# A program order planned by one clock per engine, PSUM banks held by hand, and ScalarE's reads moved, in a stack of four graph layers

## The chip, the cores and the metric

The kernel runs on one core of one Trainium2 chip. A core has five engines that work side by side, each through its own instruction stream in order: TensorE (PE in the profile, its weight loads PEld) multiplies matrices and writes to PSUM, an accumulation memory of eight banks; VectorE (DVE), ScalarE (ACT) and GpSimd (POOL) work element by element; SyncE (SP) starts transfers. All but PSUM data lies in the on-chip memory SBUF. The metric is the device time of one execution in microseconds (us), the median of several runs. Everything is float32.

## The reference, cut to what matters

There are 64 batches of 256 nodes with 128 features, and one 256 x 256 matrix `adj`. Each of four layers normalises its input over the features, takes the positive part, and adds the layer's result to its input.

```python
def _L0_gnn_ref(input, in_matrix, out_matrix, ...):          # both matrices are adj
    def step(h, _):
        m_in = einsum('nm,bmd->bnd', in_matrix, h); m_out = einsum('nm,bmd->bnd', out_matrix, h)
        av = concatenate([m_in, m_out], -1)
        u3 = h @ u3_w.T + u3_b
        z = sigmoid(av @ w3_w.T + w3_b + u3)
        r = sigmoid(av @ w4_w.T + w4_b + u3)
        hv = tanh(av @ w5_w.T + w5_b + (r * h @ u5_w.T + u5_b))
        return (1.0 - z) * h + z * hv, None
    # ... five steps
def _L1_gnn_ref(X, A1, A2, Theta1, bias):                    # both matrices are adj
    # x1 = A^T x0, x2 = 2 A^T x1 - x0 for each matrix
    # ... out = relu([X, x1, x2, x1, x2] @ Theta1 + bias)
def _L2_gnn_ref(x, adj, weight, bias):
    y = einsum('bnf,fo->bno', einsum('nm,bmf->bnf', adj, x) + x, weight) + bias
    return y / maximum(sqrt(sum(y * y, 2)), EPS)
def _L3_gnn_ref(x, W, b_lin, a, bias):                       # W and bias are adj
    s1 = einsum('bkf,ef->bke', x, W[:, :F]); s2 = einsum('bkf,ef->bke', x, W[:, F:])
    pre = s1[:, :, None, :] + s2[:, None, :, :] + b_lin
    h = where(pre >= 0, pre, ALPHA * pre)
    e = einsum('bije,e->bij', h, a) + bias
    return sigmoid(einsum('bij,bjf->bif', softmax(e, 2), x))
# each layer: h = maximum(layernorm(x), 0); x = x + layer(h)
```

The last layer is by far the largest: `pre` has 256 x 256 x 256 elements for each batch, one for every pair of nodes and every one of 256 features.

## The kernel before

Two batches, a pair, are worked on together; there are 32 pairs. The last layer of a pair takes 64 slots. In a slot n, four rows i of each half of the nodes are handled with all nodes j, for the 256 features in two blocks of 128. The first block's `max(s2, -s1)` comes from VectorE (`rl_v`). The second block's `relu(s1 + s2)` comes in two of three slots as a sum on GpSimd and a relu on ScalarE (`rl_g`), and in every third slot from eight activations on ScalarE (`rl_s`). TensorE multiplies each of them by the vector `a` (`scores`) into one PSUM bank per half pair.

```python

    def make_sum(n):
        if n >= NPAIR * SLOTS or n % 3 == 0:
            return
        ops = READY[where(n)[0]]
        TILES[n, 1] = relu_pool.tile([P, 4, NB, N], F32, name="rl_g", bufs=6)
        nc.gpsimd.tensor_add(TILES[n, 1], *operands(n, ops[4], ops[6]))
    def make(n):
        if n >= NPAIR * SLOTS:
            return
        p, ic, r = where(n)
        ops = READY[p]
        if ops[5] is None:
            ops[5] = ps_s.tile([P, NB, N], F32, name="s2a")
            project(ops[5], [(adj_t[:, 1, 0:P], ops[2])])
        TILES[n, 0] = relu_pool.tile([P, 4, NB, N], F32, name="rl_v", bufs=5)
        nc.vector.tensor_tensor(TILES[n, 0], *operands(n, ops[3], ops[5]), op=OP.max)
        if n % 3:
            t = TILES[n, 1].rearrange("p g b n -> p (g b n)")
            nc.scalar.activation(t, t, AF.Relu)
        else:
            TILES[n, 1] = relu_pool.tile([P, 4, NB, N], F32, name="rl_s", bufs=2)
            for g in range(4):
                for b in range(NB):
                    i = ic * P + g * 32 + r
                    nc.scalar.activation(TILES[n, 1][:, g, b, :], ops[6][:, b, :], AF.Relu,
                                         bias=ops[4][:, b, i:i + 1], scale=1.0)
    def scores(n):
        p, ic, r = where(n)
        if r == 0:
            PE[0] = ps_e.tile([P, NB, N], F32, name="pe")
            project(PE[0], [(g2, READY[p][2])], stop=False)
        for k in range(NE):
            rl = TILES.pop((n, k))
            for g in range(4):
                nc.tensor.matmul(flat(PE[0])[g * 32:(g + 1) * 32, :], win[:, k, 31 - r:63 - r], flat(rl[:, g]),
                                 start=False, stop=(r == 31 and k == NE - 1), skip_group_check=True)
```

While a pair goes through its slots, the layers before it of the next two pairs are computed a step at a time (`front`), and its softmax and output afterwards (`tail`). These are generators: each `yield` ends a step and gives its rough work on TensorE, VectorE and ScalarE.

```python
    def inverse_root(t, op, value):
        nc.gpsimd.tensor_scalar(t, t, value, None, op0=op)
        nc.gpsimd.tensor_tensor(t, t, minus_half, op=OP.pow)
    def norm(src, h):
        stats = work.tile([P, NB * NC, 6], F32, name="stats")
        mv = work.tile([P, NB * NC, 2], F32, name="mv")
        s = src.rearrange("p b c d -> p (b c) d")
        for k in range(NB * NC):
            nc.vector.bn_stats(stats[:, k, :], s[:, k, :])
        for k in range(NB * NC):
            nc.vector.bn_aggr(mv[:, k, :], stats[:, k, :])
        yield 0, 1.3, 0
        inverse_root(mv[:, :, 1], OP.add, LN_EPS)
        yield 0, 0, 0
        pn = bank([P, NB * NC, D], "pn")
        for k in range(NB * NC):
            nc.vector.tensor_scalar(pn[:, k, :], s[:, k, :], mv[:, k, 0:1], mv[:, k, 1:2],
                                    op0=OP.subtract, op1=OP.mult)
        yield 0, 1.6, 0
        nc.scalar.activation(h.rearrange("p b c d -> p (b c) d"), pn, AF.Relu)
        yield 0, 0, 0.6
    # ...
    def side_by_side(o, w, t, start, stop):
        for g in range(0, P, 32):
            nc.tensor.matmul(o[g:g + 32], w[:, g:g + 32], t, start=start, stop=stop, skip_group_check=True)
    def project(pp, pairs, start=True, stop=True):
        for k, (w, t) in enumerate(pairs):
            side_by_side(flat(pp), w, flat(t), start and k == 0, stop and k == len(pairs) - 1)
        return pp
    # ... front(p): norm(x0), then the first layer
        for step in range(STEPS):
            if step:
                pm = mix_nodes(h, adj_t, "pm")
                yield 1.9, 0, 0
                mT = feat("mT", **SHORT)
                nc.scalar.copy(mT, pm)
                yield 0, 0, 0.6
            pr = project(bank([P, NB, N], "pr"), [(u3t, hT), (w4t, mT)])
            yield 1.9, 0, 0
            r = bank([P, NB, N], "r")
            nc.scalar.activation(r, pr, AF.Tanh, bias=br, scale=0.5)
            yield 0, 0, 0.65
            rh = feat("rh", **SHORT)
            nc.vector.scalar_tensor_tensor(rh, r, 1.0, hT, op0=OP.add, op1=OP.mult)
            project(pr, [(w34, mT)], start=False)
            yield 0.9, 0.7, 0
            nc.scalar.activation(pr, pr, AF.Tanh, bias=bz, scale=0.5)
            pv = project(bank([P, NB, N], "pv"), [(w5t, mT), (u5t, rh)])
            yield 1.9, 0, 0.65
            nc.scalar.activation(pv, pv, AF.Tanh, bias=bh, scale=1.0)
            yield 0, 0, 0.65
            d = feat("d", **SHORT)
            nc.vector.tensor_sub(d, pv, hT)
            yield 0, 0.7, 0
            nc.vector.scalar_tensor_tensor(pr, pr, 1.0, d, op0=OP.add, op1=OP.mult)
            hT_new = feat("hT", bufs=4)
            nc.vector.scalar_tensor_tensor(hT_new, pr, 0.5, hT, op0=OP.mult, op1=OP.add)
            hT = hT_new
            yield 0, 1.4, 0
            pt = to_token(hT, "pt")
            yield 0.6, 0, 0
            if step < STEPS - 1:
                h = tok("h", **SHORT)
                # ... copy to h; then x1 and the second layer
        pt = to_feature(h, "pt")
        yield 0.6, 0, 0
        hT = feat("hT", bufs=4)
        nc.scalar.copy(hT, pt)
        pm = mix_nodes(h, adj_n, "pm")
        yield 1.9, 0, 0.6
        c1T = feat("c1T", **SHORT)
        nc.scalar.copy(c1T, pm)
        yield 0, 0, 0.6
        pt = to_token(c1T, "pt")
        yield 0.6, 0, 0
        c1 = tok("c1", **SHORT)
        nc.scalar.copy(c1, pt)
        yield 0, 0, 0.6
        pm = mix_nodes(c1, adj_n, "pm")
        yield 1.9, 0, 0
        c2T = feat("c2T", **SHORT)
        nc.vector.scalar_tensor_tensor(c2T, pm, 2.0, hT, op0=OP.mult, op1=OP.subtract)
        yield 0, 0.7, 0
        po = project_token([(hT, th[:, 0, :]), (c1T, th[:, 1, :]), (c2T, th[:, 2, :])], "po")
        # ... the third layer; then the projections for the fourth
        p1 = project(bank([P, NB, N], "p1"), [(adj_t[:, 0, P:2 * P], hT)])
        p2 = project(bank([P, NB, N], "p2"), [(adj_t[:, 1, P:2 * P], hT)])
        yield 1.9, 0, 0
        s2b = feat("s2b")
        nc.scalar.copy(s2b, p2)
        s1b = feat("s1b")
        nc.scalar.activation(s1b, p1, AF.Identity, bias=blin[:, 1:2], scale=1.0)
        yield 0, 0, 1.3
        p1 = project(bank([P, NB, N], "p1"), [(adj_t[:, 0, 0:P], hT)])
        yield 0.9, 0, 0
        s1n = feat("s1n")
        nc.scalar.activation(s1n, p1, AF.Identity, bias=nblin[:, 0:1], scale=-1.0)
        READY[p] = [x3, h3, hT, s1n, s1b, None, s2b]
```

What stands where in the program is decided slot by slot. A step is put in when it is late against an even pace, or when its work fits under three levels that each slot drains. PSUM comes from pools: five banks that circulate, one for `s2a`, two for the scores.

```python
    ps = ctx.enter_context(tc.tile_pool(name="ps", bufs=5, space=PSUM))
    ps_s = ctx.enter_context(tc.tile_pool(name="ps_s", bufs=1, space=PSUM))
    ps_e = ctx.enter_context(tc.tile_pool(name="ps_e", bufs=2, space=PSUM))
    # ...
    RATE, ROOM = (1.1, 0.65, 0.6), (2.7, 1.8, 1.5)
    level = [0.0, 0.0, 0.0]
    def fits(work):
        return all(l + w <= r or w == 0 for l, w, r in zip(level, work, ROOM))
    def charge(work):
        for k in range(3):
            level[k] += work[k]
    def background(n):
        p, k = n // SLOTS, n % SLOTS + 1
        total = len(WORK)
        room = SLOTS - SUM_AHEAD - 3
        due = {p + 1: half + (total - half) * min(1.0, k / room), p + 2: half * k / SLOTS}
        due = {q: d for q, d in due.items() if q < NPAIR and q not in READY}
        late = {q: d - FRONTS.get(q, (0, 0))[1] for q, d in due.items()}
        if k >= room and p + 1 in late:
            while p + 1 not in READY:
                charge(step(p + 1))
            late.pop(p + 1)
        if tails:
            t = tails[0]
            if n - t[1] > 2 * t[2] + 2 or n - t[1] > 2 * t[2] and fits(t[3]):
                work = next(t[0], None)
                if work is None:
                    tails.pop(0)
                else:
                    charge(work)
                    t[2:] = [t[2] + 1, work]
                in_order()
        for q in sorted(late, key=lambda q: -late[q]):
            work = WORK[FRONTS.get(q, (0, 0))[1]]
            if late[q] > 6 or late[q] > -4 and fits(work):
                charge(step(q))
        for k in range(3):
            level[k] = max(0.0, level[k] - RATE[k])
    # ...
    for n in range(NPAIR * SLOTS):
        background(n)
        make_sum(n + SUM_AHEAD)
        make(n + AHEAD)
        in_order()
        scores(n)
        in_order()
        if n % 32 == 31:
            p, ic, _ = where(n)
            tails.append([tail(p, ic, PE[0], *READY[p][:2]), n, 0, (0, 0.7, 0)])
```

Of the kernel before, what the change touches and what calls it, by code (L numbers as in the profile page):

```python
# [15 lines left out]
NB = 2  # L16
# [4 lines left out]
ENGINES = (mybir.EngineType.PE, mybir.EngineType.DVE, mybir.EngineType.Activation, mybir.EngineType.Pool)  # L21
# [6 lines left out]
def kernel(  # L28
# [49 lines left out]

    nc = tc.nc
# [9 lines left out]
    ps = ctx.enter_context(tc.tile_pool(name="ps", bufs=5, space=PSUM))  # L89
    ps_s = ctx.enter_context(tc.tile_pool(name="ps_s", bufs=1, space=PSUM))  # L90
    ps_e = ctx.enter_context(tc.tile_pool(name="ps_e", bufs=2, space=PSUM))

    def bank(shape, name):
        return ps.tile(shape, F32, tag="bank", name=name)
# [46 lines left out]

    def load_transposed(w, name, scale=None):
# [39 lines left out]
    nc.vector.tensor_copy(th[:, 0, :], th_raw[:, 0, :])  # L182
    nc.vector.tensor_add(th[:, 1:3, :], th_raw[:, 1:3, :], th_raw[:, 3:5, :])

# [38 lines left out]
    def norm(src, h):  # L223

        stats = work.tile([P, NB * NC, 6], F32, name="stats")
        mv = work.tile([P, NB * NC, 2], F32, name="mv")
        s = src.rearrange("p b c d -> p (b c) d")
        for k in range(NB * NC):
            nc.vector.bn_stats(stats[:, k, :], s[:, k, :])  # L229
        for k in range(NB * NC):  # L230
            nc.vector.bn_aggr(mv[:, k, :], stats[:, k, :])  # L231
        yield 0, 1.3, 0
        inverse_root(mv[:, :, 1], OP.add, LN_EPS)
        yield 0, 0, 0
        pn = bank([P, NB * NC, D], "pn")
        for k in range(NB * NC):
            nc.vector.tensor_scalar(pn[:, k, :], s[:, k, :], mv[:, k, 0:1], mv[:, k, 1:2],  # L237
                                    op0=OP.subtract, op1=OP.mult)
        yield 0, 1.6, 0
        nc.scalar.activation(h.rearrange("p b c d -> p (b c) d"), pn, AF.Relu)  # L240
        yield 0, 0, 0.6

    def to_feature(h, name):

        pt = bank([P, NB, NC, P], name)
        for b in range(NB):
            for c in range(NC):
                nc.tensor.transpose(pt[:, b, c, :], h[:, b, c, :], ident)
        return pt.rearrange("p b c n -> p b (c n)")

    def to_token(ht, name):

        pt = bank([P, NB, NC, P], name)
        for b in range(NB):
            for c in range(NC):
                nc.tensor.transpose(pt[:, b, c, :], ht[:, b, c * P:(c + 1) * P], ident)  # L256
        return pt

    def mix_nodes(h, a, name):

        pm = bank([P, NB, N], name)
        for b in range(NB):
            for c in range(NC):
                side_by_side(pm[:, b, :], h[:, b, c, :], a[:, c, :], c == 0, c == NC - 1)
        return pm
# [4 lines left out]
    def side_by_side(o, w, t, start, stop):  # L270

        for g in range(0, P, 32):
            nc.tensor.matmul(o[g:g + 32], w[:, g:g + 32], t, start=start, stop=stop, skip_group_check=True)  # L273

    def project(pp, pairs, start=True, stop=True):

        for k, (w, t) in enumerate(pairs):
            side_by_side(flat(pp), w, flat(t), start and k == 0, stop and k == len(pairs) - 1)
        return pp

    def project_token(pairs, name):

        pp = bank([P, NB, NC, D], name)
        for b in range(NB):
            for c in range(NC):
                for k, (t, w) in enumerate(pairs):
                    nc.tensor.matmul(pp[:, b, c, :], t[:, b, c * P:(c + 1) * P], w,
                                     start=(k == 0), stop=(k == len(pairs) - 1))
        return pp
# [6 lines left out]

    SHORT = dict(tag="short", bufs=14)

    def add_row(po, row):

        t = po.rearrange("p b c d -> p (b c) d")
        nc.vector.tensor_add(t, t, row.unsqueeze(1).to_broadcast([P, NB * NC, D]))
# [3 lines left out]
    def front(p):  # L306

        x0 = XIN.pop(p)
# [3 lines left out]
        yield from norm(x0, h)  # L312
        pt = to_feature(h, "pt")
        yield 0.6, 0, 0
        hT = feat("hT", bufs=4)
        nc.scalar.copy(hT, pt)
        pm = mix_nodes(h, adj_t, "pm")
        yield 1.9, 0, 0.6
        mT = feat("mT", **SHORT)
        nc.scalar.copy(mT, pm)  # L320
        yield 0, 0, 0.6
        for step in range(STEPS):
            if step:
                pm = mix_nodes(h, adj_t, "pm")
                yield 1.9, 0, 0
                mT = feat("mT", **SHORT)
                nc.scalar.copy(mT, pm)
                yield 0, 0, 0.6
            pr = project(bank([P, NB, N], "pr"), [(u3t, hT), (w4t, mT)])
            yield 1.9, 0, 0  # L330
            r = bank([P, NB, N], "r")
            nc.scalar.activation(r, pr, AF.Tanh, bias=br, scale=0.5)  # L332
            yield 0, 0, 0.65
            rh = feat("rh", **SHORT)
            nc.vector.scalar_tensor_tensor(rh, r, 1.0, hT, op0=OP.add, op1=OP.mult)  # L335
            project(pr, [(w34, mT)], start=False)
            yield 0.9, 0.7, 0
            nc.scalar.activation(pr, pr, AF.Tanh, bias=bz, scale=0.5)
            pv = project(bank([P, NB, N], "pv"), [(w5t, mT), (u5t, rh)])
            yield 1.9, 0, 0.65  # L340
            nc.scalar.activation(pv, pv, AF.Tanh, bias=bh, scale=1.0)
            yield 0, 0, 0.65

            d = feat("d", **SHORT)
            nc.vector.tensor_sub(d, pv, hT)  # L345
            yield 0, 0.7, 0
            nc.vector.scalar_tensor_tensor(pr, pr, 1.0, d, op0=OP.add, op1=OP.mult)  # L347
            hT_new = feat("hT", bufs=4)
            nc.vector.scalar_tensor_tensor(hT_new, pr, 0.5, hT, op0=OP.mult, op1=OP.add)  # L349
            hT = hT_new  # L350
            yield 0, 1.4, 0
            pt = to_token(hT, "pt")
            yield 0.6, 0, 0
            if step < STEPS - 1:
                h = tok("h", **SHORT)
                nc.scalar.copy(h, pt)  # L356
                yield 0, 0, 0.6
        x1 = tok("x1")
        nc.vector.tensor_add(x1, x0, pt)
        yield 0, 0.7, 0  # L360
# [3 lines left out]
        yield from norm(x1, h)  # L364
        pt = to_feature(h, "pt")
        yield 0.6, 0, 0
        hT = feat("hT", bufs=4)
        nc.scalar.copy(hT, pt)
        pm = mix_nodes(h, adj_n, "pm")
        yield 1.9, 0, 0.6  # L370
        c1T = feat("c1T", **SHORT)
        nc.scalar.copy(c1T, pm)
        yield 0, 0, 0.6
        pt = to_token(c1T, "pt")
        yield 0.6, 0, 0
        c1 = tok("c1", **SHORT)
        nc.scalar.copy(c1, pt)
# [261 lines left out]
```

## Time and profile before

| | |
|---|---|
| time, median of 3 runs | 5768.48 us (5767.91 to 5768.98) |
| span of the profiled execution | 5767.0 us |
| mean granted TensorE clock | 0.985 |
| GpSimd: 1365 sums `rl_g`, 3624 ns each | 4907.8 us busy |
| VectorE: 2048 `rl_v`, 2280 ns each | 4580.8 us busy |
| VectorE: 512 `pn` (the end of the norm), 412 ns each | 210.9 us busy |
| ScalarE: 1365 relus `rl_g`, 1923 ns each | 2588.1 us busy |
| ScalarE: 5464 activations `rl_s`, 516 ns each | 2262.3 us busy |
| ScalarE: 128 relus `h` from `pn`, 597 ns each | 76.5 us busy |

Busy time is the time in which at least one instruction of a group runs. Successive instructions of an engine overlap at their ends, so a mean length is longer than what one instruction costs; the distance between starts tells that. The lengths of TensorE's matmuls are modelled.

In the profile's lines an entry such as `L504 DVE TENSOR_TENSOR rl_v<-s2a,s1n` is a line of the kernel, an engine, an operation, and what is written from what. A wait is put down to the instruction whose end released it.

### The profile page before, as it was taken

Reading aid. Unit: us, or ns where it says so; the run is one execution under the profiler, and the core shown is the slowest. Engines: PE = TensorE matmul, PEld = TensorE weight load, DVE = VectorE, ACT = ScalarE, POOL = GpSimd, SP = SyncE. Lnnn points to the kernel's source line nnn. Section 1 sums busy time; section 2 is a strip of 40 time slices with the busy share of each in tenths; the row PEclk is TensorE's granted clock in tenths of the full one; section 3 lists DMA queues with packets and bytes.
Section 4 is the critical chain, followed back from the end, with each engine's and each line's share of the span. In section 5 each row is a group of like instructions: output and inputs, shape, how many; then the busy total and the mean of one; then the engine's idle time right before and its main releaser. Section 6 shows DMA issues by size and latency. Waiting matters only on the chain.

```text
span 5767.0 us, 121947 instructions
## 1 busy us (share of the span) xinstructions
PE 5395.0 (94%) x51853; PEld 1880.1 (33%) x51853; DVE 5482.7 (95%) x4766; ACT 5432.0 (94%) x8494; POOL 5179.1 (90%) x1819
## 2 busy tenths in 40 slices
PE   6899999999999999999999999999999999999988
PEld 2333333333333333333333333333333333333322
DVE  3999999999999999999999999999999999999998
ACT  2999999999999999999999999999999999999999
POOL 0999899999999999999998999989989999999998
PEclk9999999999999999999999999999999999999999
DMA  0000000000000000000000000000000000000000
GB/s 17 4 4 5 2 5 5 4 5 5 2 5 5 4 5 2 5 5 4 5 5 2 5 5 4 5 2 5 5 4 5 5 2 5 5 3 3 2 3 4
DMA packets 38739, 25.90 MB, mean 4 GB/s; under 512 B 3505, under 2 KB 38193, under 8 KB 38193
## 3 DMA queue, kind: packets, MB, share of 16 engines
q1 hardware_dynamic: 35088, 17.05, 1.0%
q8 instruction: 406, 6.65, 0.5%
q10 hardware_dynamic: 3104, 1.05, 0.1%
q14 instruction: 141, 1.15, 0.1%
HBM read 9.70 MB, written 8.39 MB: 3 GB/s over the span
## 4 chain that ended last, share of the span: by engine, by line
DVE 54%; PE 24%; ACT 11%; issue 7%; POOL 3%; DMA 0%; ACTq 0%; POOLq 0%; SPq 0%; DVEq 0%
DVE rl_v L504 41%; PE pe L525 14%; ACT rl_s L513 4%; ACT rl_g L507 4%; PE pm L273 3%; DVE pn L237 3%; PE pr L273 2%; POOL rl_g L493 2%; PE p L273 2%; DVE stats L229 1%; DVE hT L349 1%; DVE rh L335 1%; DVE d L345 1%; DVE pr L347 1%; PE pt L256 1%
## 5 line engine op out<-in xcount | busy, mean ns | idle before, releaser
L493 POOL TENSOR_TENSOR rl_g<-s2b,s1b 128x2048 f32<-128x2048 f32 x1365 | 4907.8, 3624 | 292.3 <-PE pe L525 243.0
L504 DVE TENSOR_TENSOR rl_v<-s2a,s1n 128x2048 f32<-128x2048 f32 x2048 | 4580.8, 2280 | 118.7 <-ACT r L332 47.0
L507 ACT ACTIVATE rl_g<-rl_g 128x2048 f32<-128x2048 f32 x1365 | 2588.1, 1923 | 3.3 <-POOL rl_g L493 3.3
L513 ACT ACTIVATE rl_s<-s2b,s1b 128x256 f32<-128x256 f32 x5464 | 2262.3, 516 | 26.8 <-PE pe L525 26.8
L525 PE MATMUL pe<-rl_v,win 128*32 128x512 f32 x16384 | 2165.8, 598 | 1.6 <-DVE rl_v L504 1.6
L525 PE MATMUL pe<-rl_g,win 128*32 128x512 f32 x10920 | 1424.8, 594 | 1.8 <-ACT rl_g L507 1.8
L525 PEld LDWEIGHTS pe<-rl_v,win 128*32 128x32 f32 x16384 | 498.4, 110 | 974.6 <-issue 859.1
L525 PE MATMUL pe<-rl_s,win 128*32 128x512 f32 x5464 | 731.7, 596 | 0.0
L525 PEld LDWEIGHTS pe<-rl_g,win 128*32 128x32 f32 x10920 | 352.7, 110 | 831.4 <-issue 756.1
L273 PE MATMUL pm<-adj_t,h 128*32 128x256 f32 x5120 | 313.0, 386 | 32.6 <-ACT h L356 32.0
L525 PEld LDWEIGHTS pe<-rl_s,win 128*32 128x32 f32 x5464 | 182.1, 111 | 426.0 <-issue 392.1
L256 PE MATMUL pt<-ident,hT 128*128 128x128 f32 x640 | 105.7, 289 | 159.9 <-DVE hT L349 159.9
L220 POOL TENSOR_SCALAR mv<-mv 128x4 f32<-128x4 f32 x128 | 29.7, 232 | 233.9 <-DVE mv L231 231.4
L273 PEld LDWEIGHTS pm<-adj_t,h 128*32 128x32 f32 x5120 | 163.1, 111 | 226.2 <-ACT h L356 76.4
L273 PE MATMUL p<-hT,adj_t 128*32 128x512 f32 x768 | 120.6, 776 | 63.0 <-ACT hT L424 63.0
L237 DVE TENSOR_SCALAR pn<-x,mv 128x128 f32<-128x128 f32 x384 | 158.2, 412 | 15.0 <-POOL mv L221 4.4
L273 PE MATMUL pr<-mT,w 128*32 128x512 f32 x1280 | 167.5, 595 | 3.6 <-ACT r L332 3.6
L273 PE MATMUL pr<-hT,u3t 128*32 128x512 f32 x1280 | 167.8, 596 | 0.0
L273 PE MATMUL pr<-mT,w4t 128*32 128x512 f32 x1280 | 167.2, 594 | 0.0
L273 PE MATMUL pv<-mT,w5t 128*32 128x512 f32 x1280 | 166.6, 592 | 0.0
L273 PE MATMUL pv<-rh,u5t 128*32 128x512 f32 x1280 | 166.6, 592 | 0.0
L256 PEld LDWEIGHTS pt<-ident,hT 128*128 128x128 f32 x640 | 69.1, 144 | 296.3 <-issue 214.2
(113 smaller groups left out, 3422.1 us busy)
## 6 DMA issues: line engine op xcount, KB each, us to landing
xin<-in_x_dram SPq DMA_DIRECT2D x64, 128.0 KB, 2.3
out_dram<-o SPq DMA_DIRECT2D x64, 128.0 KB, 1.8
w_raw<-in_L_gnn_w_w_dram ACTq DMA_DIRECT2D x3, 128.0 KB, 2.5
th_raw<-in_L_gnn_Theta_dram ACTq DMA_DIRECT2D x1, 320.0 KB, 3.2
adj_n<-in_adj_dram SPq DMA_DIRECT2D x1, 256.0 KB, 4.5
w_raw<-in_L_gnn_u_w_dram ACTq DMA_DIRECT2D x2, 64.0 KB, 2.3
bias<-in_L_gnn_bias_dram ACTq DMA_DIRECT2D x2, 64.0 KB, 3.6
w<-in_L_gnn_weight_dram ACTq DMA_DIRECT2D x1, 64.0 KB, 2.9
```

The costliest lines, as they stand in the source:

```text
L229: nc.vector.bn_stats(stats[:, k, :], s[:, k, :])
L237: nc.vector.tensor_scalar(pn[:, k, :], s[:, k, :], mv[:, k, 0:1], mv[:, k, 1:2], op0=OP.subtract, op1=OP.mult)
L256: nc.tensor.transpose(pt[:, b, c, :], ht[:, b, c * P:(c + 1) * P], ident)
L273: nc.tensor.matmul(o[g:g + 32], w[:, g:g + 32], t, start=start, stop=stop, skip_group_check=True)
L335: nc.vector.scalar_tensor_tensor(rh, r, 1.0, hT, op0=OP.add, op1=OP.mult)
L345: nc.vector.tensor_sub(d, pv, hT)
L347: nc.vector.scalar_tensor_tensor(pr, pr, 1.0, d, op0=OP.add, op1=OP.mult)
L493: nc.gpsimd.tensor_add(TILES[n, 1], *operands(n, ops[4], ops[6]))
L504: nc.vector.tensor_tensor(TILES[n, 0], *operands(n, ops[3], ops[5]), op=OP.max)
L507: nc.scalar.activation(t, t, AF.Relu)
L513: nc.scalar.activation(TILES[n, 1][:, g, b, :], ops[6][:, b, :], AF.Relu, bias=ops[4][:, b, i:i + 1], scale=1.0)
L525: nc.tensor.matmul(flat(PE[0])[g * 32:(g + 1) * 32, :], win[:, k, 31 - r:63 - r], flat(rl[:, g]), start=False, stop=(r == 31 and k == NE - ...
```

## The change

It has four parts.

1. The program is planned with a clock for each engine. Each step says which engine it begins on and when its input will be there; it is put in when that engine's planned clock has reached this time (or when it is over eight steps late). The clocks know the buffers of the tiles too.
2. The eight PSUM banks are one tile each. Two hold s2 for VectorE (`s2a`) and, new, a copy of the other block's s2 for ScalarE (`s2p`); two hold scores; four circulate, and the plan takes the one that is free first.
3. The end of the norm moves from VectorE to ScalarE: four activations with the scale 1/deviation and the bias -mean/deviation, which GpSimd works out, in place of four VectorE operations and one relu. ScalarE's `rl_s` reads s2 from PSUM.
4. The second hop of the second layer is computed as `2 adj adj` applied to h, with the subtraction of x0 folded into the weights, instead of from the first hop's result. The step of the second hop needs no turned copy of the first.

The diff, cut to its core (what is left out renames helpers, adapts the remaining steps in the same manner, or holds the loop that starts the first two pairs):

```diff
+    psum = ctx.enter_context(tc.tile_pool(name="psum", bufs=1, space=PSUM))
+    banks = [psum.tile([P, NB * N], F32, name=f"bank{k}") for k in range(8)]
+    s2a, s2p = (b.rearrange("p (b n) -> p b n", b=NB) for b in banks[:2])
+    pes = banks[2:4]
+    clock = dict.fromkeys((PE, DVE, ACT, POOL), 0.0)
+    SEEN = {PE: 0.25, DVE: 0.14, ACT: 0.15, POOL: 0.13}
+    def ran(engine, us, *after):
+        clock[engine] = max(clock[engine], 0.0, *after) + us
+        return clock[engine] + SEEN[engine]
+    spare = [[b, 0.0] for b in banks[4:]]
+    def take():
+        spare.sort(key=lambda b: b[1])
+        return spare.pop(0)
 ...
+    adj_2 = const.tile([P, NC, N], F32, name="adj_2")
+    for c in range(NC):
+        pt = bank([P, N], "pt")
+        for k in range(NC):
+            nc.tensor.matmul(pt, adj_t[:, k, c * P:(c + 1) * P], adj_n[:, k, :], start=(k == 0), stop=(k == NC - 1))
+        nc.vector.tensor_scalar(adj_2[:, c, :], pt, 2.0, None, op0=OP.mult)
 ...
+    nc.vector.tensor_sub(th[:, 0, :], th_raw[:, 0, :], th[:, 2, :])
 ...
+    PROJECT, MIX, TURN, PRODUCT, PRODUCTS = 0.86, 1.74, 0.69, 1.18, 2.99
+    COPY, BIASED, TANH, ELEMENTS = 0.48, 0.58, 0.57, 0.61
 ... norm
-        for k in range(NB * NC):
-            nc.vector.tensor_scalar(pn[:, k, :], s[:, k, :], mv[:, k, 0:1], mv[:, k, 1:2],
-                                    op0=OP.subtract, op1=OP.mult)
-        nc.scalar.activation(h.rearrange("p b c d -> p (b c) d"), pn, AF.Relu)
+        nc.gpsimd.tensor_scalar(mv[:, :, 0], mv[:, :, 0], -1.0, None, op0=OP.mult)
+        nc.gpsimd.tensor_mul(mv[:, :, 0], mv[:, :, 0], mv[:, :, 1])
+        t = ran(POOL, 1.6, t)
+        yield ACT, t
+        for k in range(NB * NC):
+            nc.scalar.activation(h[:, k, :], s[:, k, :], AF.Relu, bias=mv[:, k, 0:1], scale=mv[:, k, 1:2])
+        return ran(ACT, 1.54, t)
 ... a step of the first layer
+            yield PE, t_h, 1
+            b = take()
+            mix_nodes(b[0], h, adj_t)
+            t = ran(PE, MIX, t_h, b[1])
+            yield ACT, t
+            mT, t_m = copied("mT", b, t)
 ... second layer
-        pt = to_token(c1T, "pt")
-        c1 = tok("c1", **SHORT)
-        nc.scalar.copy(c1, pt)
-        pm = mix_nodes(c1, adj_n, "pm")
-        c2T = feat("c2T", **SHORT)
-        nc.vector.scalar_tensor_tensor(c2T, pm, 2.0, hT, op0=OP.mult, op1=OP.subtract)
+        mix_nodes(b[0], h, adj_2)
+        t = ran(PE, MIX, t_h, b[1])
+        yield ACT, t
+        c2T, t = copied("c2T", b, t)
 ... make
-        nc.vector.tensor_tensor(TILES[n, 0], *operands(n, ops[3], ops[5]), op=OP.max)
+        nc.vector.tensor_tensor(tile_, *operands(n, ops["s1n"], s2a), op=OP.max)
+        TILES[n, 0] = tile_, ran(DVE, 2.2, ops["t_2a"], ops["t_n"], t_free["v"].pop(0))
 ...
+            if "t_2p" not in ops:
+                nc.scalar.copy(s2p, ops["s2b"])
+                ops["t_2p"] = ran(ACT, COPY, ops["t_b"])
-                    nc.scalar.activation(TILES[n, 1][:, g, b, :], ops[6][:, b, :], AF.Relu,
-                                         bias=ops[4][:, b, i:i + 1], scale=1.0)
+                    nc.scalar.activation(tile_[:, g, b, :], s2p[:, b, :], AF.Relu,
+                                         bias=ops["s1b"][:, b, i:i + 1], scale=1.0)
+            TILES[n, 1] = tile_, ran(ACT, 2.86, t_free["s"].pop(0))
 ... background
+    def wait_of(key):
+        engine, since, *bank = CHAINS[key][1]
+        if bank:
+            if not spare:
+                return 1e9
+            since = max(since, min(b[1] for b in spare))
+        return since - clock[engine]
 ...
+                late = -late
+                if late < -AHEAD_STEPS:
+                    continue
+                wait = wait_of(key)
+                if wait <= TOLERANCE or late > LATE and wait < 100 or key == p + 1 and k >= room:
+                    break
+            else:
+                return
+            advance(key)
+    AHEAD_STEPS, TOLERANCE, LATE = 15, 0.05, 8
```

## The prediction

> **What bounds the kernel now.** I read the busy line of the page first, then busy time over a steady stretch, then the waits in that stretch, then single instructions in order of time. The page's first part:
>
> ```profile
> PE 5395.0 (94%) x51853; PEld 1880.1 (33%) x51853; DVE 5482.7 (95%) x4766; ACT 5432.0 (94%) x8494; POOL 5179.1 (90%) x1819
> ```
>
> Four engines are at 90 to 95%, so no single one can be relieved alone. The order of the program repeats every three pairs of batches (a pair has 64 slots, and every third slot has a ScalarE tile), so I took six pairs, 1058.13 us, as the stage to reason in. Busy time by engine (columns: the stretch and its length; PE, PEld, DVE, ACT, POOL; granted clock, DMA share, GB/s), and below it some of the waits in that stretch (engine, line, releaser: us in total, times, longest):
>
> ```profile
> 3360.44:4418.57 1058.13, 1002.52 (x9724) 350.56 (x9720) 1025.98 (x889) 1017.32 (x1593) 971.28 (x341) 0.99 0.02 4
> ```
> ```profile
> POOL rl_g L493 <- PE pe L525: 47.0, 38, 4.5
> PE pt L256 <- DVE hT L349: 29.4, 18, 2.3
> ...
> ACT s2b L430 <- PE p L273: 16.4, 6, 3.8
> ...
> DVE rl_v L504 <- ACT r L332: 9.4, 4, 2.4
> ```
>
> Divided by six: a pair takes 176.36 us, of which VectorE (DVE) works 171.0, ScalarE (ACT) 169.6, TensorE (PE) 167.1, GpSimd (POOL) 161.9. VectorE is the bound, with 5.4 us a pair of waiting. GpSimd's waits are for buffers that TensorE has still to read, a consequence of the others. TensorE's and ScalarE's waits come from background steps (the layers of the next two pairs) that stand in the program before their input is there: all TensorE waits for DVE hT, for example.
>
> The rest is the two ends. The rows of the s2a projection, one per pair, start between 144.1 and 5601.7 us: 31 periods of 176.05 us, 144 us before them, and 165.3 us from the last to the end at 5767.0.
>
> **Pitch.** Neighbouring instructions overlap in the records, so I cost by the distance between starts:
>
> ```profile
> 5706.25 3.29 ACT L513 ACTIVATE rl_s<-s2b,s1b 128x256 f32<-128x256 f32 x8
> 5709.44 3.70 ACT L507 ACTIVATE rl_g<-rl_g 128x2048 f32<-128x2048 f32 x2
> 5713.04 3.29 ACT L513 ACTIVATE rl_s<-s2b,s1b 128x256 f32<-128x256 f32 x8
> ```
> ```profile
> 4001.00 1.76 DVE L237 TENSOR_SCALAR pn<-x,mv 128x128 f32<-128x128 f32 x4
> 4002.66 4.48 DVE L504 TENSOR_TENSOR rl_v<-s2a,s1n 128x2048 f32<-128x2048 f32 x2
> 4007.06 0.68 DVE L345 TENSOR_TENSOR d<-pv,hT 128x512 f32<-128x512 f32 x1
> ```
>
> Eight rl_s take 3.19 us (0.40 each), one rl_g on ScalarE 1.80, four pn 1.66, one rl_v 2.20. The same reading gives 0.60 for a 128x512 VectorE operation, 0.48 for a ScalarE copy out of PSUM, 0.86 for a set of eight 128x512 matmuls, 1.73 for a mix over the nodes, 0.6 to 0.7 for four transposes.
>
> [...] the trace shows 3.19/8 = 399. [...] no 256-wide PSUM read stands in this trace. [...] ScalarE stands idle 16.4 us (six times) for p although relu tiles follow, and sets of matmuls with a length of 1.04 start 0.86 apart. [...]
>
> **The change part by part, in us per pair.**
>
> 1. *s2 from PSUM.* A pair has 21.3 ScalarE tiles of eight activations. [...] a tile from 3.19 to 2.86, which is also the constant in the new planner. 21.3 x 0.33 = 7.0 off ScalarE. One copy of s2b a pair puts 0.5 back.
>
> 2. *Norm moved.* Four norms a pair each lose four pn (1.66): 6.6 off VectorE. ScalarE's one 128x512 relu (0.50) becomes four 128x128 activations with scale and bias from memory. [...] the planner charges 1.54, and since the trace's biased 128x512 activations cost 0.1 more than plain ones I take 1.54. That is +1.04 x 4 = 4.2 on ScalarE. GpSimd gets two 128x4 operations more: the one in the trace lasts 0.23, the planner charges 0.35 for both; +1.4.
>
> 3. *The second hop by a squared matrix.* Off: four transposes on TensorE (0.7) and the c2T operation on VectorE (0.6). ScalarE loses the c1 copy and gains the c2T copy: nothing. The mix stays. The hop no longer waits for the first hop's copy, transpose and copy; that shortens a chain which lies beside the slots, so it pays only at the start. The squared matrix costs a few matmuls once.
>
> 4. *Order and banks.* No work is added or taken. Four banks circulate instead of five, since one goes to the copy of s2. A step is put into an engine's program when its input should be there by that engine's planned time, instead of by levels of work. This is aimed at the waits above.
>
> Sums: VectorE 171.0 - 6.6 - 0.6 = 163.8 (adding the pitches of all its operations I get 164.5). ScalarE 169.6 - 7.0 + 0.5 + 4.2 = 167.3 (by pitches 166.3). TensorE by pitches: 64 x 2 x 0.86 = 110.1 for the scores, 31 sets of 0.86 = 26.7, eight mixes = 13.9, ten groups of transposes = 6.9, products 6.5: 164.1. GpSimd 161.9 + 1.4 = 163.3.
>
> So the largest load falls from 171.0 to about 166.5, and the bound passes from VectorE to ScalarE, with TensorE 2 to 3 us behind. If the waiting stayed at 5.4 a pair, the period would be 172; if the planner took all of it, 166.5. Four loads within 3 us of each other cannot be run without loss through buffers of two to six tiles, but the planner knows those buffers: I take 2.7, half of the waiting, left. Period 169.2.
>
> Ends: the start is one long chain for pair 0, in which pair 1 gets every second step; now pair 1 fills only where pair 0 would wait, and the two hops stand side by side. In the trace a step of the first layer takes about 14 us against some 12.5 of pure chain, so perhaps 10 us come off: 134. The last pair has no background and 42.7 GpSimd sums of 3.58 (153 us) set its length, which does not change: 165.
>
> 134 + 31 x 169.2 + 165 = 5544, say **5545 us**, a ratio of 0.961.
>
> **The rivals.**
>
> A. *ScalarE becomes the bound and gives little.* If the read from PSUM saves less than 42 ns, or 128x128 activations cost more than 0.385, ScalarE stays near 169.6 or above: with a tile at 3.19 again it would be 174.3, and with the old waiting there would be no gain at all. For it: ScalarE is the new bound on paper. Against it: a 128x512 PSUM copy has a pitch of 0.48 and a 2048-wide SBUF relu 1.80[...]. Half the saving lost: 3.5 x 31 = +110, 5650.
>
> B. *Steps wait for their turn and are then forced.* ScalarE works four tiles ahead of TensorE. A chain that goes TensorE, ScalarE, TensorE waits for that lead each time, some 25 to 30 times a front; at 8 to 10 us each this is most of the two periods (350 us) that a front has. Steps that come more than eight behind are put in regardless of the wait, and then TensorE stands still as now, with only 3 us of slack instead of 9; four banks instead of five add to it. Then waiting is 6 to 8 a pair: a period of 173 to 174, 5665 to 5690. For it: TensorE's waits for hT, 29.4 us in six pairs. Against it: the planner counts banks and buffers in its clock, the old rule knew neither.
>
> C. *The plan works nearly fully.* Waiting of 1 us: period 167.3, 5485.
>
> **Range and chances.** 5470 is the period at 166.8, 5650 that at 172.6: A half true, or the waiting as before. Faster by over 2% means below 5653, that is, a period below about 172.7. Only A in full or B brings it above; slower than 5884 would need a period of 180, more than any sum here. Faster 0.87, within 2% 0.11, slower 0.02.
>
> **What would show it.** Right: rl_s at a pitch near 0.36; VectorE near 164 and ScalarE 166 to 167 busy us per pair over six pairs; no pn rows; waits of TensorE for hT and h well below 10 us a pair in all; first slot before 140 us. Wrong on step 1: rl_s still at 0.40. On step 2: norm activations at 0.45 or more. On step 4: TensorE or ScalarE waits above 5 us a pair in which relu tiles were ready, or rl_v waiting for buffers. What would break the number most is a shared limit that no row shows[...]: rl_v above 2.20.

## The result and the profile after

The changed kernel takes **5566.47 us** (median of 4 runs, 5561.99 to 5567.5) against 5768.73 before, a ratio of 0.9648 with a 95% interval of 0.9631 to 0.9665. The prediction said 5545 with a range of 5470 to 5650. The page's busy line, and the same six-pair stretch as before (pairs 12 to 17; PE, PEld, DVE, ACT, POOL, then granted clock, DMA share, GB/s):

```profile
PE 5364.9 (96%) x51733; PEld 1876.4 (34%) x51733; DVE 5273.8 (95%) x4224; ACT 5390.2 (97%) x8910; POOL 5222.9 (94%) x2075
```
```profile
2180.33:3198.20 1017.87, 992.43 (x9700) 348.22 (x9696) 986.40 (x786) 1009.21 (x1673) 979.66 (x389) 0.99 0.02 5
```

A pair takes 1017.87 / 6 = 169.6 us, in place of 176.4. VectorE is busy 164.4 us a pair, 6.6 less than before, and no longer the busiest: ScalarE is, with 168.2. That figure must be read with care, as the three ScalarE groups that the change touches show (count, then busy us, mean ns, and the idle time before them):

```profile
L625 ACT ACTIVATE rl_g<-rl_g 128x2048 f32<-128x2048 f32 x1365 | 2846.3, 2198 | 19.0 <-POOL rl_g L608 18.7
L635 ACT ACTIVATE rl_s<-bank,s1b 128x256 f32<-128x256 f32 x5464 | 2226.4, 730 | 41.2 <-PE bank L649 40.1
...
L331 ACT ACTIVATE h<-x,mv 128x128 f32<-128x128 f32 x384 | 166.5, 581 | 11.8 <-POOL mv L327 11.7
```

The mean rl_s became longer, 730 ns for 516, though it is started more often: its distance from start to start is 356 ns, where it was 399. Even rl_g, the same instruction as before, reads 2198 ns for 1923 at an unchanged distance of 1800. ScalarE's ends are recorded later, and its busy time with them. So the loads below are sums of starts: for each kind of instruction, the distance to the next start that it has when nothing holds the engine up (the lower quartile), times its count, over 18 pairs. ScalarE's load is then 166.7 us a pair, of which 1.4 is the one copy of s2. Some 0.9 of that is in truth a wait of the next instruction for the copy (below).

The waits of the changed kernel in the six pairs (engine, line, releaser: us in total, times, longest):

```profile
PEld bank L259 <- DVE rl_v L620: 28.2, 12, 4.6
POOL rl_g L608 <- PE bank L649: 27.3, 14, 3.4
PE bank L259 <- DVE rl_v L620: 21.0, 6, 3.7
...
DVE rl_v L620 <- PE bank L649: 15.8, 16, 2.0
...
DVE rl_v L620 <- PE bank L259: 8.9, 6, 2.1
ACT rl_s L635 <- PE bank L649: 7.7, 8, 2.0
```

TensorE's wait for hT, 29.4 us before, is gone from the head of the list, and so is ScalarE's for p. In their place stands one wait a pair, 3.5 us each: line 259, here the projection of s2a. Its bank can be written only when VectorE has read it for the last time in the pair before. TensorE at that place in the changed kernel, in order of time (start, length, wait in brackets), and then VectorE:

```profile
2344.46 1.04 PE L649 MATMUL bank<-rl_g,win 128*32 128x512 f32 x8
2348.66 1.06 PE L259 MATMUL bank<-hT,adj_t 128*32 128x512 f32 x8 [3.15 <-DVE rl_v L620]
```
```profile
2344.12 4.48 DVE L620 TENSOR_TENSOR rl_v<-bank,s1n 128x2048 f32<-128x2048 f32 x2
2349.79 2.29 DVE L620 TENSOR_TENSOR rl_v<-bank,s1n 128x2048 f32<-128x2048 f32 x1 [1.19 <-PE bank L259]
```

TensorE stands until VectorE's tiles end at 2348.6, projects, and VectorE then stands 1.19 us for it.

One wait grew. VectorE waits for tile buffers that TensorE has still to read 15.8 us in six pairs; in the six pairs of the kernel before it was

```profile
DVE rl_v L504 <- PE pe L525: 7.6, 7, 2.5
```

### The profile page after: what moved, and what is told of

Its sections match the earlier page's. It is cut to its first block, busy times and chain, and to the rows that moved or that the text cites. A ratio compares the mean times of both kernels' runs of the same rounds, so it can differ in the third digit from the quotient of the medians.

```text
span 5560.2 us, 122022 instructions
## 1 busy us (share of the span) xinstructions
PE 5364.9 (96%) x51733; PEld 1876.4 (34%) x51733; DVE 5273.8 (95%) x4224; ACT 5390.2 (97%) x8910; POOL 5222.9 (94%) x2075
## 3 DMA queue, kind: packets, MB, share of 16 engines
q14 instruction: 145, 1.19, 0.1%
## 4 chain that ended last, share of the span: by engine, by line
PE 56%; DVE 20%; ACT 16%; issue 6%; POOL 2%; DMA 0%; ACTq 0%; DVEq 0%; POOLq 0%; SPq 0%
PE bank L649 35%; DVE rl_v L620 16%; PE bank L259 16%; ACT rl_g L625 7%; ACT rl_s L635 6%; POOL rl_g L608 2%; PE bank L295 2%; PE bank L287 2%; PE bank L564 1%; ACT h L331 1%; DVE bank L404 1%; PE bank L280 1%; DVE d L400 1%; DVE hT L408 1%; DVE stats L320 0%
## 5 line engine op out<-in xcount | busy, mean ns | idle before, releaser
L620 DVE TENSOR_TENSOR rl_v<-bank,s1n 128x2048 f32<-128x2048 f32 x2048 | 4576.9, 2280 | 151.9 <-PE bank L649 89.8
L625 ACT ACTIVATE rl_g<-rl_g 128x2048 f32<-128x2048 f32 x1365 | 2846.3, 2198 | 19.0 <-POOL rl_g L608 18.7
L635 ACT ACTIVATE rl_s<-bank,s1b 128x256 f32<-128x256 f32 x5464 | 2226.4, 730 | 41.2 <-PE bank L649 40.1
L649 PE MATMUL bank<-rl_v,win 128*32 128x512 f32 x16384 | 2187.9, 599 | 12.0 <-DVE rl_v L620 11.6
L649 PE MATMUL bank<-rl_g,win 128*32 128x512 f32 x10920 | 1434.4, 595 | 14.3 <-ACT rl_g L625 14.3
L649 PEld LDWEIGHTS bank<-rl_v,win 128*32 128x32 f32 x16384 | 514.1, 110 | 1068.2 <-issue 933.2
L649 PE MATMUL bank<-rl_s,win 128*32 128x512 f32 x5464 | 754.5, 595 | 0.5 <-ACT rl_s L635 0.5
L649 PEld LDWEIGHTS bank<-rl_g,win 128*32 128x32 f32 x10920 | 352.5, 111 | 858.4 <-issue 710.6
L259 PE MATMUL bank<-adj_t,h 128*32 128x256 f32 x5120 | 309.5, 382 | 7.4 <-ACT h L419 7.4
L331 ACT ACTIVATE h<-x,mv 128x128 f32<-128x128 f32 x384 | 166.5, 581 | 11.8 <-POOL mv L327 11.7
L259 PE MATMUL bank<-rh,u5t 128*32 128x512 f32 x1280 | 168.2, 592 | 0.0
L395 ACT ACTIVATE bank<-bank,gate_b 128x512 f32<-128x512 f32 x160 | 156.5, 978 | 11.6 <-PE bank L259 11.2
L259 PE MATMUL bank<-hT,u3t 128*32 128x512 f32 x1280 | 166.7, 593 | 0.0
L259 PE MATMUL bank<-mT,w4t 128*32 128x512 f32 x1280 | 166.7, 592 | 0.0
L377 ACT ACTIVATE bank<-bank,gate_b 128x512 f32<-128x512 f32 x160 | 152.1, 951 | 13.2 <-PE bank L259 13.0
```

Source lines behind the costliest of these rows:

```text
L331: nc.scalar.activation(h[:, k, :], s[:, k, :], AF.Relu, bias=mv[:, k, 0:1], scale=mv[:, k, 1:2])
L377: nc.scalar.activation(r[0], pr[0], AF.Tanh, bias=br, scale=0.5)
L395: nc.scalar.activation(pv[0], pv[0], AF.Tanh, bias=bh, scale=1.0)
L620: nc.vector.tensor_tensor(tile_, *operands(n, ops["s1n"], s2a), op=OP.max)
L635: nc.scalar.activation(tile_[:, g, b, :], s2p[:, b, :], AF.Relu, bias=ops["s1b"][:, b, i:i + 1], scale=1.0)
L649: nc.tensor.matmul(pe[g * 32:(g + 1) * 32, :], win[:, k, 31 - r:63 - r], flat(tile_[:, g]), start=False, stop=(r == 31 and k == NE - 1), s ...
```

## The experiments

The theory: the largest load sets the period, the plan takes part of the waiting; by the expectation for the moves alone (below), some 110 us of the gain would be the moves of work and 90 the plan. The rivals: the plan makes the gain whatever the loads, or the moves make it alone. In the table, the largest load and the period are us per pair; the waiting is their difference. TensorE is not among the loads, since its lengths are modelled; by busy time it has 165.4 us a pair in the changed kernel, close below ScalarE.

| kernel | time, us | largest load | period | waiting |
|---|---|---|---|---|
| before | 5768.73 | DVE 171.0 | 176.4 | 5.4 |
| changed | 5566.47 | ACT 166.7 | 169.6 | 2.9 |
| a_sbuf: changed, s2 from SBUF | 5717.99 | ACT 172.2 | 174.7 | 2.5 |
| a_normdve: changed, norm on VectorE | 5730.18 | DVE 171.2 | 175.0 | 3.8 |
| a_oldhop: changed, hop from hop | 5625.95 | ACT 166.6 | 171.8 | 5.2 |
| a_plan: plan alone | 5738.97 | DVE 171.9 | 175.0 | 3.1 |
| b_moves: moves alone | 5883.13 | ACT 166.7 | 180.2 | 13.5 |
| b_moves_l2: moves, old rule with one number changed | 5654.81 | ACT 166.0 | 172.6 | 6.6 |
| b_s2p: before, s2 from PSUM alone | 5760.65 | DVE 171.0 | 176.4 | 5.4 |
| b_norm: before, norm on ScalarE alone | 5836.96 | ACT 172.6 | 178.6 | 6.0 |
| b_4banks: before, four banks | 5768.75 | DVE 171.0 | 176.4 | 5.4 |

**Undoing one move each in the changed kernel.** s2 from SBUF:

```diff
-                nc.scalar.copy(s2p, ops["s2b"])
 ...
-                    nc.scalar.activation(tile_[:, g, b, :], s2p[:, b, :], AF.Relu, ...
-            TILES[n, 1] = tile_, ran(ACT, 2.86, t_free["s"].pop(0))
+                    nc.scalar.activation(tile_[:, g, b, :], ops["s2b"][:, b, :], AF.Relu, ...
+            TILES[n, 1] = tile_, ran(ACT, 3.19, t_free["s"].pop(0))
```

> The changed kernel with ScalarE's 21.3 tiles a pair reading s2 from SBUF again (no copy into PSUM, planner told 3.19). Theory (the largest load sets the period, the plan only takes part of the waiting): ScalarE's load goes from 166.7 to 166.7 - 1.4 + 170.7 x 0.043 = 172.6 us a pair, and with 2 to 2.9 of waiting the period is 174.6 to 175.5, so 5735 to 5765 us: nearly the whole gain is gone. Rival (the plan makes the gain, loads matter little): 5570 to 5620.

Measured 5717.99, below the theory's range of times, though the period of 174.7 lies in its range of periods, and about 100 us above the rival's. The load rose by 5.5 us a pair and the period by 5.1. The waiting is 0.4 less; that the others have more slack when ScalarE alone is slowed would explain it, but is not shown.

The end of the norm on VectorE again, through a circulating bank:

```diff
+        yield DVE, t, 1
+        b = take()
 ...
+            nc.vector.tensor_scalar(pn[:, k, :], s[:, k, :], mv[:, k, 0:1], mv[:, k, 1:2], ...)
+        t = ran(DVE, 1.66, t, b[1])
 ...
+        nc.scalar.activation(h, pn, AF.Relu)
 ...
-            nc.scalar.activation(h[:, k, :], s[:, k, :], AF.Relu, bias=mv[:, k, 0:1], scale=mv[:, k, 1:2])
```

> The changed kernel with the end of the norm on VectorE again. Theory of loads: VectorE 163.4 + 6.6 = 170.0 us a pair, ScalarE 162.5; period 171.5 to 172.9, so 5640 to 5685 us. Rival (the plan makes the gain): 5570 to 5600. A third view (ScalarE was the real bound, so its relief by 4.2 us counts): below 5566.

Measured 5730.18, more than expected: the load is 171.2 for the 170.0 expected, the waiting is 3.8, and the first slot comes at 164.2 us, 17 later than in the changed kernel. In that start ScalarE stands 28.0 us in all for VectorE's end of the norm, between 98 and 165 us. The third view is out: ScalarE's relief by 5 us bought nothing.

The second hop from the first one again:

```diff
-        mix_nodes(b[0], h, adj_2)
 ...
-        c2T, t = copied("c2T", b, t)
 ...
+        to_token(b[0], c1T)
 ...
+        nc.scalar.copy(c1, by_token(b[0]))
 ...
+        mix_nodes(b[0], c1, adj_n)
 ...
+        nc.vector.scalar_tensor_tensor(c2T, by_feature(b[0]), 2.0, hT, op0=OP.mult, op1=OP.subtract)
```

> The changed kernel with the second hop computed from the first one again, and no squared matrix. Theory of loads: TensorE 0.7 and VectorE 0.6 more a pair, neither of them the largest load; period up by 0 to 0.7, the start 3 us shorter at its setup and some 3 longer in its chain: 5560 to 5590 us. Rival (the longer chain makes steps late and they are forced): 1 to 2 us a pair, 5600 to 5630.

Measured 5625.95, inside the rival's range. The largest load is that of the changed kernel, yet the period is 2.2 us longer and the first slot 7.6 us later. The chain of a front is three stations longer, and the edit as a whole costs waiting. Whether the chain's length does it, or the places where the steps come to stand, or TensorE, whose busy time rises from 165.4 to 167.4 us a pair, was not separated.

**The moves and the plan alone.** All three moves with the old rule, and, next, the plan with none of them (the three diffs above at once):

```diff
-    ps = ctx.enter_context(tc.tile_pool(name="ps", bufs=5, space=PSUM))
+    ps = ctx.enter_context(tc.tile_pool(name="ps", bufs=4, space=PSUM))
 ...
+            ops.append(ps_s.tile([P, NB, N], F32, name="s2p"))
+            nc.scalar.copy(ops[7], ops[6])
 ...
+            nc.scalar.activation(hr[:, k, :], s[:, k, :], AF.Relu, bias=mv[:, k, 0:1], scale=mv[:, k, 1:2])
+            if k % 2:
+                yield 0, 0, 0.77
 ...
+        pm = mix_nodes(h, adj_2, "pm")
```

> The kernel before, with its old rule for the order, and with all three moves of work (s2 from PSUM, norm on ScalarE, squared matrix; four circulating banks). Theory of loads: the largest load is 166.7, the waiting stays at 5.4 a pair, period 172.1, so about 5660 us: of the gain of 202 us the moves bring 110 and the plan 90. Rival (the plan makes the gain): 5700 or more. Rival (the moves alone make it): 5570 to 5600.

> The new order of the program alone: the changed kernel with all three moves of work undone (rl_s from SBUF, end of the norm on VectorE, second hop from the first). VectorE's load is about 171.5 us a pair again and ScalarE's 168.5. Theory (the plan cuts the waiting wherever the load lies; 2.9 to 3.8 a pair in the runs so far): period 174.4 to 175.5, about 5720 to 5760 us. Rival (the plan and the moves only work together): 5768 or more.

The moves alone made the kernel *slower* than before, 5883.13: ratio 1.0201 (1.0184 to 1.0218). That is within the letter of the rival's "5700 or more", but none of the three views had the moves as a loss. The plan alone takes 5738.97, 0.9947 (0.9931 to 0.9964). So -30 and +114 stand against -202 together: the parts do not add.

Three parts of this edit followed, each alone on the kernel before: s2 from PSUM (the first four changed lines of the diff), the norm (the next three, five banks), and four banks (the first two):

> The kernel before with rl_s reading a copy of s2 in PSUM, alone (so four circulating banks). ScalarE falls to about 163 us a pair, VectorE stays the largest with 171.0. If the loads decide: 5760 to 5770 us. If the fifth bank is what the old order misses in the run with all moves (13.5 us of waiting a pair): 5800 to 5880.

> The kernel before with the end of the norm on ScalarE, alone, five circulating banks. VectorE falls to 164.4 us a pair, ScalarE rises to 172.5. If the loads decide, with the waiting of 5.4: period 178, 5825 us. If the old order fits the moved norm badly (ScalarE's instructions placed before their input is there): 5880 or more.

> The kernel before with four circulating PSUM banks in place of five and nothing else. If banks in rotation are what cost the old order its waiting in the run with all moves: 5810 to 5880 us. If not: 5768 to 5780.

s2 from PSUM takes 6 us of load off ScalarE and leaves the period as it was, since VectorE bounds; 5760.65 is 0.9985 (0.9978 to 0.9992). The norm alone gives 5836.96: it relieves VectorE and makes ScalarE the bound at 172.6. To the kernel before, the fifth bank is worth nothing, 5768.75. Each follows the loads with the old waiting. Only all moves together do not, and the time in each eighth of a pair (by the starts of the rl_v tiles) tells where some of it goes: the last eight slots take 23.0 us before, 28.2 in b_norm and 27.4 in b_moves. So b_norm has the slow stretch too, and that its waiting is still near the old one does not show that the loads alone set its time. One such stretch of b_moves (length, then busy us of the five engines, clock, DMA), and ScalarE's instructions in it in order of time:

```profile
2459.60:2487.90 28.30, 21.57 (x192) 6.53 (x192) 19.66 (x13) 24.08 (x40) 24.82 (x8) 0.94 0.01 1
```
```profile
2464.25 0.57 ACT L426 COPY hT<-pt 128x512 f32<-128x512 f32 x1
2468.44 0.58 ACT L432 COPY s2b<-p 128x512 f32<-128x512 f32 x1 [3.62 <-PE p L280]
2468.92 0.69 ACT L434 ACTIVATE s1b<-p,blin 128x512 f32<-128x512 f32 x1
2470.21 0.69 ACT L439 ACTIVATE s1n<-p,nblin 128x512 f32<-128x512 f32 x1 [0.60 <-PE p L280]
2470.80 0.65 ACT L348 ACTIVATE pv<-pv,gate_b 128x512 f32<-128x512 f32 x1
```

The longest waits around it, of the same kernel:

```profile
...
DVE d L352 <- ACT pv L348: 7.4, 1, 7.4
ACT s2b L432 <- PE p L280: 3.6, 1, 3.6
POOL rl_g L495 <- PE pe L530: 3.5, 2, 2.8
PEld pt L255 <- ACT h L246: 3.3, 3, 2.3
```

The old rule puts all steps that are still missing into the program at slot 54 (`k >= room`). Each of them waits for the one before on another engine. In ScalarE's queue the next front's pv stands behind s1n; VectorE's d waits 7.4 us for pv, and the relu tiles wait behind d. If this burst is the cause, fewer late steps must remove it:

```diff
-            if late[q] > 6 or late[q] > -4 and fits(work):
+            if late[q] > 2 or late[q] > -4 and fits(work):
```

> The kernel before with all three moves of work, and its old rule changed in one number: a front's step is put in regardless of room when it is 2 steps late, in place of 6. The last eight slots of a pair take 27.4 us in the run with 6 (23.0 before), and there all late steps are put in at once. If this burst is what costs: the last eight slots near 22 us, period 175 or less, below 5740 us. If any forced step costs as much wherever it stands: 5850 to 5900 us.

5654.81 us, 0.98 (0.9787 to 0.9814): one number in the old rule is worth 228 us once the moves are there. The last eight slots take 20.6 us, which is 6.8 of the 7.6 us by which the period falls, and one of these stretches of b_moves_l2, in the same columns, has TensorE and GpSimd busy all through:

```profile
2369.70:2390.20 20.50, 20.50 (x204) 6.21 (x196) 19.11 (x11) 19.59 (x33) 20.50 (x7) 1.00 0.00 1
```

So the burst was the cause of most of the loss. The moves together with this number bring 114 us, and the plan 88 more, close to the split that the theory gave. It is no clean split: the number was not tried in the kernel before, with its 5.4 us of waiting, so what it brings without the moves is not shown. And the waiting is 6.6 here where the theory took 5.4, so part of the agreement is luck.

**What is left.** Two waits at the edge of a pair, and the end. First the copy of s2, which ScalarE reads at once and so waits for, in the changed kernel (columns are start and length), and the edit that moves it:

```profile
2010.26 2.65 ACT L625 ACTIVATE rl_g<-rl_g 128x2048 f32<-128x2048 f32 x1
2012.06 1.33 ACT L629 COPY bank<-s2b 128x512 f32<-128x512 f32 x1
2013.43 3.03 ACT L635 ACTIVATE rl_s<-bank,s1b 128x256 f32<-128x256 f32 x8
2016.30 3.76 ACT L625 ACTIVATE rl_g<-rl_g 128x2048 f32<-128x2048 f32 x2
```
```diff
             TILES[n, 1] = tile_, ran(ACT, 2.86, t_free["s"].pop(0))
+            m = next_s(n)
+            if m < NPAIR * SLOTS and m // SLOTS > p:
+                copy_s2(READY[p + 1])
```

> The changed kernel with ScalarE's copy of s2 into PSUM placed one or two tiles earlier, right behind the last rl_s of the pair before, so that ScalarE does not stand waiting for its own copy (distance to the next start 1.31 to 1.61 us there, against 0.47 for a copy). If that wait is a loss on the bounding engine: 0.9 us a pair off, about 5538 us. Rival: the wait is also where ScalarE's late ends (up to 1.4 us behind, by the records of rl_s) are worked off; without it they grow on from pair to pair, others wait longer, and the time stays at 5566 or rises.

5562.32, 0.9642 (0.9629 to 0.9655): no change that can be told from the changed kernel. The rival's time came, but not by its mechanism, as ScalarE at the edge of a pair in this kernel shows:

```profile
3020.36 3.69 ACT L641 ACTIVATE rl_s<-bank,s1b 128x256 f32<-128x256 f32 x8
3024.09 0.59 ACT L615 COPY bank<-s2b 128x512 f32<-128x512 f32 x1
3024.61 1.91 ACT L632 ACTIVATE rl_g<-rl_g 128x2048 f32<-128x2048 f32 x1
```

The copy no longer holds up the reads behind it, but it overwrites what the eight rl_s ahead of it read, and waits for their late end at 3024.05. The wait moved to the other side of the copy: 1.25 us from the last rl_s to the copy in place of 0.36. A copy between the two rl_g tiles was not tried.

The s2a projection two slots later:

```diff
-        make(n + AHEAD)
+        edge = (n // SLOTS + 1) * SLOTS
+        make_v(edge - 1 if n < edge - HELD and n + AHEAD >= edge else n + AHEAD)    # HELD = 2
```

> The changed kernel with the first rl_v tiles of a pair, and the s2a projection ahead of them, put two slots later into the programs of VectorE and TensorE, so that TensorE does the scores of two more slots before it waits for VectorE's last read of the old s2a (3.4 us a pair in the changed kernel). If this wait costs time: up to 1.5 us a pair off, about 5520 us. Rival (TensorE has that slack, and VectorE now stands idle at the edge instead): 5560 to 5590 us; the planner's own clock says +0.2 us a pair.

5552.35, 0.9622 (0.9609 to 0.9636). The period is 0.3 us shorter. All four times (5549.59 to 5552.64) lie below the four of the changed kernel (5561.99 to 5567.5), though the intervals of the two ratios just overlap: a small gain is likely, and neither account's range holds. The wait did not go away. Between 2000 and 4000 us TensorE waited 41.0 us for VectorE at the projection in the changed kernel; now it waits 35.7 for rl_v at the scores.

A version that aims beyond both kernels:

```diff
-            tile_ = relu_pool.tile([P, 4, NB, N], F32, name="rl_s", bufs=2)
+            tile_ = relu_pool.tile([P, 4, NB, N], F32, name="rl_s", bufs=3)
 ...
-    SHORT = dict(tag="short", bufs=14)
+    SHORT = dict(tag="short", bufs=12)
 ...
-        return "s" if n % 3 == 0 else "g"
+        return "s" if n % 3 == 0 or n >= (NPAIR - 2) * SLOTS and n % 15 == 1 else "g"
```

> The changed kernel with the copy of s2 placed early, a third buffer for rl_s tiles (paid with two of the 14 short buffers), and in the last two pairs, where there is little background work and GpSimd is the slowest, every fifteenth slot's tile made by ScalarE in place of GpSimd where it was GpSimd's. The planner's clock says 0.9 us a pair for the buffer and 10 us for the end; with 0.9 a pair for the copy: about 5505 us. If late ends of ScalarE eat the copy's share: 5530.

**5521.69 us**, 0.957 (0.9557 to 0.9583), the fastest of all, between the two times expected. It has the early copy of a_early too, which alone left the period at 169.6; with the third buffer the period is 168.4 and ScalarE's recorded idle time 0.3 us a pair in place of 1.5. The end, from the last pair's first rl_v on, is 162.0 us for 170.8. The copy's share is missing, probably for the reason above; the parts were not run apart.

## Why the prediction was right, and where it was not

**The period** was predicted as 169.2; it is 169.6 in the steady pairs and 169.1 over all. Its parts:

- *s2 from PSUM.* An rl_s takes 356 ns by starts where it took 399 from SBUF, so eight take 2.85 us for the 2.86 predicted. The 2.86 is the planner's constant and was an estimate: no trace of the kernel before showed it. The copy was put at 0.5 us and takes 1.4, because rl_s waits for its end (the copy above ends at 2013.39, and rl_s starts at 2013.43).
- *Norm.* An activation takes 384 ns by starts; the planner's figure, which the prediction took, was 385. VectorE's load fell to 163.4 (predicted 163.8). GpSimd rose by the predicted 1.4 in busy time (161.9 to 163.3), but by 2.4 in starts: its power operation beside the new ones takes 1.11 us for 1.01, and the three small ones 0.78 together.
- *Waiting.* "Half of the waiting, left" was a choice of 2.7; that it is 2.9 is luck. With the copy of s2 at the 0.5 us that was charged, the wait behind it counts as waiting too: then the load is 165.8, 0.7 below the 166.5 predicted, and the waiting 3.8.

**Step 3, the hop, was wrong.** It "pays only at the start", the prediction said. Undone, it costs 59 us, and 2.2 us a pair are in the steady part. So the shorter chain, with the places that its steps take, is worth something beside the slots, even where the largest load does not change. Rival B named a possible reason (every trip from engine to engine waits for a lead); which part does it stays open.

**The ends** were too short in the prediction. By its own mark, the s2a projection, the start is 145.5 us for 134 and the end 172.2 for 165, some 19 us in all, of which the periods give 3 back. The rest of the 21 us between 5545 and 5566 lies between the profiled execution's span of 5560.2 and the median time. The first rl_v starts at 146.9 us. The squared matrix and what hangs on it start the first norm at 23.98 us, 2.9 later than before. And pair 1 did not merely fill gaps: the copies mT of pair 0 in the changed kernel, in order of time, show a step of the first layer every 14.8 to 15.0 us,

```profile
33.01 0.59 ACT L337 COPY mT<-bank 128x512 f32<-128x512 f32 x1 [1.67 <-PE bank L259]
...
47.96 0.59 ACT L337 COPY mT<-bank 128x512 f32<-128x512 f32 x1 [2.05 <-PE bank L259]
...
62.77 0.59 ACT L337 COPY mT<-bank 128x512 f32<-128x512 f32 x1 [2.05 <-PE bank L259]
```

for the 12.5 assumed, with both pairs in step. In the end, GpSimd's 43 sums take 156.4 us without a pause (156.5 in the kernel before), near the predicted 153. But the first of them starts 0.5 us ahead of the last pair's first rl_v, where it was 8.8 before. The lost lead, 8.3 us, is about what the end grew by, 7.6 us to 170.8 by rl_v; why it was lost was not tried. The first two periods, 157.3 and 181.1, make 169.2 on average: pair 1's early work came back as nothing.

**Of what was to be seen**, the pitch, the loads and the vanished waits came. The sign for TensorE's waits was weak, as the 29.4 us for hT before were already 4.9 a pair. "First slot before 140 us" did not come, and the wait for s2a was not foreseen. The shared limit that the prediction feared did not show: rl_v starts 2.20 us apart in both kernels. One sign against step 4, "rl_v waiting for buffers", did show: 2.6 us a pair for 1.3 before, on an engine that no longer sets the pace. Of rival A only the new bound came, not its costs. Rival C's waiting of 1 us was not reached. The split between moves and plan came out near only with the old rule's number changed: as that rule stood, the moves alone lose 114 us, which nothing in the sum of loads could tell.

## What to carry to other kernels

When several engines are within a few per cent of each other, a load moved is worth what the next largest load allows, and no more: 6 us a pair off ScalarE bought some 8 us of 5769 while VectorE bounded. A hand-tuned order belongs to the work it was tuned for; after moving work, look at each part of the repeating stretch for a burst, and change the order's own numbers before judging the move. A plan that knows when each input will be there still has numbers of its own (the lengths of the steps, the limits 15, 0.05 and 8); here one set of them gave a waiting of 2.5 to 5.2 us a pair whichever moves were undone. What it does not know, such as an instruction's wait for its own engine's last write (here 0.9 us a pair at the copy of s2), it cannot avoid.

## What the hardware showed that was not expected

ScalarE's ends fell behind its starts in the kernels whose rl_s reads s2 from PSUM. In the changed kernel, over 18 steady pairs, the median rl_s is recorded 712 ns long and the 95th percentile 1156, with starts 356 apart; in a_plan, where rl_s reads s2 from SBUF, the median is 508 at 399 apart. From one rl_s to the next, the end slips by a median of 8 ns (4 to 11 for nine in ten in the changed kernel). The median is 8 in each of the nine kernels whose rl_s reads PSUM, b_s2p among them, where ScalarE has 11.3 us a pair of recorded idle time, and 0 in each of the five whose rl_s reads SBUF. The slip went back a little from one rl_g to the next, by a median of 5 ns in the changed kernel, and to nothing where ScalarE waited for one of its own results: there the last rl_s before the copy of s2 is recorded 1200 ns long, and the first behind it 475 (medians; the copy at 2012.06 is 1.33 us long, and the one at 3024.09, behind such a wait, 0.59). That these ends are real and no fault of the records is shown by the waits: what needs the result starts after the late end, by 0.04 us in both copies above. What holds the ends back, and what the delay costs other engines, stays open.
